# A two-layer graph network on one core: the last two expert blocks under a condition, and the experts' outputs taken by chunks from two queues

## The chip, the core and the metric

The kernel runs on one core of a Trainium2 chip. The metric is the device time of one execution in microseconds. A core has TensorE (PE, with its weight loads as PEld), VectorE (DVE), ScalarE (ACT), GpSimd (POOL) and SyncE (SP), each with an instruction order of its own, and 16 DMA engines that SP, ACT and POOL feed through queues. SBUF is the on-chip memory of 128 partitions, PSUM the one that TensorE writes.

## The reference, cut to what matters

3125 nodes with 256 features go through two layers of a graph network with mixers and mixtures of experts. The change lies where layer 0 ends and layer 1 begins:

```python
# layer 0, expert part: x is the layer norm of the nodes, 8 experts of width 1024, the best 2 of each node
shared = gelu(x @ W1s + b1s) @ W2s + b2s
rw = softmax(x @ Wr); topw, topi = top_k(rw, 2); topw = topw / sum(topw)
mask = sum(one_hot(topi, 8) * topw[..., None], axis=-2)
priv = gelu(einsum('bsd,edf->bsef', x, W1p) + b1p) @ W2p + b2p        # per expert
x_out = x_in + shared + einsum('bsed,bse->bsd', priv, mask)
# layer 1, messages: 50000 edges, 4 heads of 64 features
xn = layernorm(x_out)
messages = (xn @ W_forward.T)[src] * dir[:, 0:1] + (xn @ W_reverse.T)[src] * dir[:, 1:2]
# attention scores per edge, softmax over the edges of a target, weighted sum per target
```

Layer 1 has a second, linear attention (called galerkin in the kernel) over the same `xn`, and a mixture of experts whose router is a graph attention over 32768 edges of its own.

## The kernel before, in words

`self.x` holds the nodes in SBUF as 25 tiles of 125 rows by 256. CHUNKS cuts the 25 tiles into seven chunks of 4, 4, 4, 4, 3, 3 and 3 tiles. The framework decides the order of instructions on each engine from a cost model and from the order of the program, except inside `tc.manual_schedule(engines=...)`, where the named engines keep the order of the program.

**Experts of layer 0** (`layer0_ffn`). A counting pass on VectorE gives every pair of node and expert a slot. Each expert's slots are rounded up to blocks of BLK = 256 rows; `nb` is the number of blocks of each expert and `end` its running sum. NBLK = 2 * 3125 // 256 + 8 = 32 blocks is what any routing can need at most. Rows are scattered to their slots in device memory. The loop over the blocks then does, for every block b:

- `block_in`: SP reads the block's expert from `exi` and loads the block's rows (L847), W1 (L848), W2 (L849) and the bias (L850); three buffers each.
- `block_hidden`: four transposes (L858), a copy to `xs` on VectorE (L859), products with W1 (L864) with a gelu on ScalarE each (L866), and some small VectorE operations that compute the weights `own` and the target rows `toi` (L870 to L884). A slot that no node uses gets a spare row as its target.
- `block_out` of the block before (or, in block 0, the last chunk of the shared expert): products with W2 (L892), the weighting `yo` on VectorE (L895), and two scatters of 128 rows into y2 in device memory on POOL (L58, told apart by their names: `y<-yo,toi`).
- `sort_columns`: eight more scatters on POOL (`sorted<-s_rows,pos`), which carry out a part of the sort of layer 1's own edges, 256 columns in all. It fills a buffer `s_rows` (L1054; 16 buffers) and writes the block's `toi` into it (L1055), which ties the scatters to the pace of the blocks.

After the loop, y2 holds for each node its two experts' outputs, in two halves of 3125 rows. For each chunk and each half SP loads the rows (L67, the helper `move`, two DMAs of 112 and 13 partitions) into one of three buffers per half, and VectorE adds them to `self.x` (L915).

**Start of layer 1** (`layer1_mix`). `layernorm` goes over the chunks: statistics on VectorE (L168, L169), Sqrt on ScalarE (L170), reciprocal and normalised rows on VectorE (L171, L178), transposes on TensorE (L183), copies to `xT` on ScalarE (L185). After that, per tile, the product of `xT` with both message weights (`token_matmul`, L191), a copy on ScalarE (L1189), and per chunk two DMAs of SP into the table `tab1` (L67, `tab<-t_st`). The message loop begins with `fetch`: POOL gathers rows of `tab1` by the edges' sources (L51, `g<-tab,t_src`), 391 gathers in groups of eight; the weights of the linear attention (`nat`, L1451) are loaded and transposed meanwhile.

Two conditionals are there before the change, L476 and L1360: paths for edges in any order, whose test `bad > 0` is false for these inputs.

Of the kernel before, what the change touches and what calls it, by code (L numbers as in the profile page):

```python
# [8 lines left out]
F32 = mybir.dt.float32  # L9
I32 = mybir.dt.int32  # L10
BF16 = mybir.dt.bfloat16
AF = mybir.ActivationFunctionType
OP = mybir.AluOpType
AX = mybir.AxisListType
PSUM = bass.MemoryType.PSUM
DRAM = bass.MemoryType.DRAM

N = 3125
D = 256
P = 125  # L20
NT = 25
# [7 lines left out]
NBLK = 2 * N // BLK + 8  # L29
# [33 lines left out]
def move(queue, out, in_):  # L63


    for s in (slice(0, 112), slice(112, P)):
        queue.dma_start(out[s], in_[s])  # L67
# [7 lines left out]
def rows_of(table):  # L75
    return table.rearrange("(t p) d -> p t d", p=P)
# [12 lines left out]
class Kernel:  # L89
# [596 lines left out]
    def layer0_ffn(self):  # L686
        nc, tc, a = self.nc, self.tc, self.a
        NE, FC = 8, 8
        with ExitStack() as c:
# [70 lines left out]
            exi = keep.tile([1, NBLK], I32, name="exi")  # L760
            nc.vector.tensor_copy(exi, exf)


# [133 lines left out]

            todo = None
            for b in range(NBLK):
                ins = block_in(b)  # L900
                nxt = block_hidden(b, *ins)
                if b == 0:
                    output(*pending)
                else:
                    block_out(*todo)
                self.sort_columns(hp, b * EC // NBLK, (b + 1) * EC // NBLK, nxt[3])
                todo = nxt
            block_out(*todo)

            for t0, n in CHUNKS:  # L910
                s = slice(t0, t0 + n)
                for i in range(2):
                    r = wp.tile([P, 4, D], F32, name=f"w{i + 1}")
                    move(nc.sync, r[:, :n, :], rows_of(self.y2[i * N:(i + 1) * N])[:, s, :])
                    nc.vector.tensor_add(self.x[:, s, :], self.x[:, s, :], r[:, :n, :])  # L915

# [132 lines left out]
    def sort_columns(self, pool, f0, f1, pace):  # L1049


        nc = self.nc
        rows = pool.tile([128, EC // NBLK, 16], I32, name="s_rows", bufs=16)
        nc.vector.tensor_copy(rows[:, :f1 - f0, :], self.src2[:, f0:f1, None].to_broadcast([128, f1 - f0, 16]))  # L1054
        nc.vector.tensor_copy(rows[:, :f1 - f0, 15], pace[:, 0:1].to_broadcast([128, f1 - f0]))  # L1055
        for f in range(f0, f1):
            self.unordered("sorted", scatter(nc, self.sorted[:], self.pos2[:, f:f + 1], rows[:, f - f0, :]))
# [110 lines left out]
    def layer1_mix(self):  # L1168
        nc, tc, a = self.nc, self.tc, self.a
        W, HD = 68, 64  # L1170
        with ExitStack() as m:
            big = m.enter_context(tc.tile_pool(name="l1", bufs=1))
            wk = m.enter_context(tc.tile_pool(name="l1w", bufs=2))
# [5 lines left out]

            xT = big.tile([128, 2, N], F32, name="xT2")  # L1180
            tab1 = self.tab1 = self.dram.tile([N, 2 * W], F32, name="tab1")
            with tc.tile_pool(name="l1l", bufs=1) as lp:
                self.layernorm(lp, ps_a, "2", xT)
            for t0, n in CHUNKS:
                st = wk.tile([P, 4, 2 * W], F32, name="t1_st")
                for i in range(n):
                    pm = ps_a.tile([P, 2 * W], F32, name="ln_pt")
                    self.token_matmul(pm, xT, t0 + i, self.wcat)
                    nc.scalar.copy(st[:, i, :], pm)  # L1189
                move(nc.sync, rows_of(tab1)[:, t0:t0 + n, :], st[:, :n, :])  # L1190

# [112 lines left out]

            E_ = mybir.EngineType
            with tc.manual_schedule(engines={E_.PE, E_.DVE, E_.Activation}):
# [38 lines left out]
            for t0, n in CHUNKS:  # L1345
                s = slice(t0, t0 + n)
                for t in range(t0, t0 + n):
                    for h in range(4):
                        xs = self.x[:, t, h * HD:(h + 1) * HD]
                        nc.vector.scalar_tensor_tensor(xs, acc[:, t, h, :HD], den[:, t, h:h + 1], xs,  # L1350
                                                       op0=OP.mult, op1=OP.add)
        self.layer1_any_order()

    def layer1_any_order(self):
# [573 lines left out]
```

## Time and profile before

| What | us |
|---|---|
| median of 3 runs (2807.82 to 2812.39) | 2810.51 |
| the profiled execution | 3210.01 |
| its span, first to last instruction | 3208.3 |
| its first block's products to its last scatter of y2 | 1293.5 to 1792.8 |
| its first load of y2 to the first gather of messages | 1794.3 to 1865.4 |
| its mean granted TensorE clock | 0.844 |

The profiled execution is about 400 us longer than the runs without a profile; durations in the text are from the profiled one. A row of a group or of the timeline gives the line, the engine, the operation, output <- inputs and shape; "[2.50 <-DVE yo L895]" means that the engine had stood idle for 2.50 us and what ended that. A queue (SPq, POOLq) is where an engine's DMAs, branches and semaphore instructions are recorded. A digit at the end of a tile's name is left out in the profile, so y2 is `y`, `xT2` is `xT`, `tab1` is `tab` and `t1_st` is `t_st`.

### The profile page before, as it was taken

The numbers are of one execution on the slowest core, as the hardware profiler recorded it, in microseconds if no ns is written. First come the engines' busy times: TensorE is split into PE (matmuls) and PEld (weight loads), VectorE is DVE, ScalarE is ACT, GpSimd is POOL, SyncE is SP. The second block draws the span as 40 slices with busy tenths as digits, with TensorE's granted clock in tenths as the row PEclk, the third lists the DMA queues.
The fourth block names the chain that finished last, engine by engine and source line by source line (L and its number), as shares of the span: only waits on it lengthen the run. The fifth ranks groups of instructions, "written<-read, shape, count | busy, mean of one in ns | idle before, by whom it ended". The sixth has DMA issues, their size and how long they took to land. (4 is left out here: it accounts for less than half of the span.)

```text
span 3208.3 us, 26947 instructions
## 1 busy us (share of the span) xinstructions
PE 2295.1 (72%) x9183; PEld 1705.1 (53%) x9183; DVE 1516.4 (47%) x3630; ACT 539.8 (17%) x1107; POOL 1640.0 (51%) x1490
## 2 busy tenths in 40 slices
PE   1753652169998699899999458798668564788773
PEld 1442431057675466788787345465546353555552
DVE  7874750065547760122111448688569810122225
ACT  1420000000000111222222124344000110122213
POOL 5887887700000170566666157777547246555612
PEclk9865765579998699999999779899878777989886
DMA  8904200034330020655554422221112210111133
GB/s 311 367 2 112 68 12 1 0 78 98 79 98 29 17 76 1 211 169 184 180 177 150 100 69 49 45 48 44 40 31 46 68 37 7 21 33 43 41 90 72
DMA packets 179585, 265.05 MB, mean 83 GB/s; under 512 B 54288, under 2 KB 143866, under 8 KB 176051
## 3 DMA queue, kind: packets, MB, share of 16 engines
q1 hardware_dynamic: 121057, 206.38, 21.1%
q0 software_dynamic: 52480, 47.70, 7.2%
q10 hardware_dynamic: 5894, 9.09, 0.8%
q8 instruction: 76, 1.25, 0.2%
q14 instruction: 78, 0.63, 0.1%
HBM read 178.73 MB, written 84.21 MB: 82 GB/s over the span
## 5 line engine op out<-in xcount | busy, mean ns | idle before, releaser
L51 POOL DMA_INDIRECT g<-tab,t_src x391 | 454.4, 1162 | 259.1 <-issue 111.4
L58 POOL DMA_INDIRECT adj<-ch_sum,ch_place x391 | 488.8, 1250 | 148.0 <-issue 119.4
L460 PE MATMUL psum<-sup,adjT 125*125 125x256 f32 x1250 | 328.2, 411 | 218.6 <-issue 164.5
L460 PEld LDWEIGHTS psum<-sup,adjT 125*125 125x125 f32 x1250 | 250.8, 203 | 285.2 <-issue 200.6
L58 POOL DMA_INDIRECT sorted<-s_rows,pos x256 | 245.9, 961 | 187.6 <-DVE s_rows L1055 119.1
L51 POOL DMA_INDIRECT G<-tabg,g_src x256 | 251.2, 981 | 159.5 <-DVE g_src L1613 83.9
L1286 PE MATMUL pw<-v,hot 128*125 128x260 f32 x1244 | 328.4, 427 | 0.0
L1286 PEld LDWEIGHTS pw<-v,hot 128*125 128x125 f32 x1244 | 259.0, 212 | 50.5
L1644 PE MATMUL fpy<-fw,fh 128*125 128x256 f32 x800 | 208.5, 418 | 86.8 <-ACT fh L1638 36.9
L864 PE MATMUL ph<-xs,w 128*128 128x256 f32 x1024 | 232.3, 385 | 33.4 <-issue 29.6
L1644 PEld LDWEIGHTS fpy<-fw,fh 128*125 128x125 f32 x800 | 164.5, 209 | 135.9 <-ACT fh L1638 43.4
L864 PEld LDWEIGHTS ph<-xs,w 128*128 128x128 f32 x1024 | 194.2, 192 | 71.3 <-issue 44.0
L892 PE MATMUL py<-w,h 128*128 128x256 f32 x1024 | 231.2, 379 | 0.0
L463 DVE TENSOR_TENSOR x<-x,psum 125x512 f32<-125x512 f32 (+1 forms) x104 | 69.1, 666 | 327.2 <-remote 169.4
L1636 PE MATMUL fph<-xT,fw 128*128 128x500 f32 (+1 forms) x448 | 181.2, 553 | 37.0 <-ACT fh L1638 34.0
L892 PEld LDWEIGHTS py<-w,h 128*128 128x128 f32 x1024 | 192.1, 190 | 24.8
L620 POOL MEMSET tier<- 125x64 f32 x1 | 0.2, 157 | 378.1 <-PE psum L460 378.1
L866 ACT ACTIVATE h<-ph,b 128x256 f32<-128x256 f32 x256 | 121.2, 474 | 392.4 <-PE ph L864 357.4
L1030 PE MATMUL pctx<-s_mv,s_ro 128*128 128x256 f32 x512 | 154.9, 413 | 1.9 <-DVE s_mv L1029 1.9
L1636 PEld LDWEIGHTS fph<-xT,fw 128*128 128x128 f32 x448 | 86.2, 195 | 111.8 <-issue 52.8
L170 ACT ACTIVATE ln_rs<-ln_mv,eps 125x4 f32<-125x4 f32 (+1 forms) x28 | 7.5, 296 | 793.0 <-DVE ln_mv L169 793.0
L1638 ACT ACTIVATE fh<-fph,cols 128x500 f32<-128x500 f32 (+1 forms) x112 | 69.5, 633 | 420.4 <-PE fph L1636 226.5
(524 smaller groups left out, 3435.7 us busy)
## 6 DMA issues: line engine op xcount, KB each, us to landing
adjT<-adj SPq DMA_DIRECT2D x25, 1367.2 KB
adj<-zero SPq DMA_DIRECT2D x22, 1536.0 KB
w<-in_L_ffn_W1p_dram SPq DMA_DIRECT2D x32, 1024.0 KB
w<-in_L_ffn_W2p_dram SPq DMA_DIRECT2D x32, 1024.0 KB
slots<-empty SPq DMA_DIRECT2D x1, 8448.0 KB
srow<-slots SPq DMA_DIRECT2D x32, 264.0 KB
adj<-ch_sum,ch_place POOLq DMA_INDIRECT x391
g<-tab,t_src POOLq DMA_INDIRECT x391
```

Of the source, the lines that this page charges most:

```text
L51: nc.gpsimd.indirect_dma_start(out=out, out_offset=None, in_=table, in_offset=bass.IndirectOffsetOnAxis(ap=idx, axis=0))
L58: return nc.gpsimd.indirect_dma_start(out=table, out_offset=bass.IndirectOffsetOnAxis(ap=idx, axis=0), in_=rows, in_offset=None, **kw)
L460: nc.tensor.matmul(pm[:, i, :], mats[b][:, (a0 + i) * P:(a0 + i + 1) * P], sup[:, b, :], start=(b == b0), stop=(b == b0 + n - 1))
L463: nc.vector.tensor_add(xs, xs, pm[:, :m, :])
L864: nc.tensor.matmul(ph, w1[:, k, f * 128:(f + 1) * 128], xs[:, k, :], start=(k == 0), stop=(k == 1))
L866: nc.scalar.activation(h[:, f, :], ph, AF.Gelu, bias=b1[:, f:f + 1])
L892: nc.tensor.matmul(py, h[:, f, i * 128:(i + 1) * 128], w2[:, f, :], start=(f == 0), stop=(f == FC - 1))
L1030: nc.tensor.matmul(p1, ro[:, f - f0, :], mv, **st)
L1286: nc.tensor.matmul(pw.rearrange("p h c -> p (h c)"), hot[:, i - i0, :], v[:, i, :, :].rearrange("p h c -> p (h c)"), start=(i == i0), stop ...
L1636: nc.tensor.matmul(ph[:, :n * P], w1[:, k, f * 128:(f + 1) * 128], xT[:, k, t0 * P:(t0 + n) * P], start=(k == 0), stop=(k == 1))
L1638: nc.scalar.activation(hs[:, f, :n * P], ph[:, :n * P], AF.Gelu, bias=self.col("L1_ffn_b1", ei * FC + f))
L1644: nc.tensor.matmul(py, hs[:, f, i * P:(i + 1) * P], w2[:, f, :], start=(f == 0), stop=(f == FC - 1))
```

## The change

- NBLK - 2 = 30 blocks run without a condition. The last two stand in `tc.If(many > 30)`, where `many` is the number of blocks that the routing needs, kept in a tile `blocks` and loaded into a register of every engine. In the conditional each block's load, hidden part and output follow each other.
- The 256 sort columns are spread over 30 blocks: the first block carries 24, the others eight, and `s_rows` is filled in pieces of eight columns.
- The loads of y2 and their sums, layer 1's norm, its transposes and the message products move into a new function `experts_in`, in which PE, DVE, ACT and SP keep the order of the program. All loads are issued ahead, one half of y2 from SP's queue and the other from ACT's, into seven buffers. Each chunk goes through sum and statistics (`moments`), and one chunk later through normalising, transposes, products and the write to `tab1` (`table`).
- The normalised rows are computed on ScalarE (Identity with scale and bias per partition) instead of VectorE.

```diff
--- before.py
+++ after.py
@@ -759,6 +759,8 @@
             nc.vector.tensor_reduce(exf, which[:, :, 1:], AX.X, OP.add)
             exi = keep.tile([1, NBLK], I32, name="exi")
             nc.vector.tensor_copy(exi, exf)
+            blocks = keep.tile([1, 1], I32, name="blocks")
+            nc.vector.tensor_copy(blocks, end[:1, NE - 1:NE])
 
 
             nc.vector.tensor_sub(run, run, cnt)
@@ -895,24 +897,26 @@
                     nc.vector.tensor_scalar(yo, py, own[:, i, 2:3], None, op0=OP.mult)
                     self.unordered("y2", scatter(nc, self.y2[:], to[:, i:i + 1], yo))
 
-            todo = None
-            for b in range(NBLK):
+
+            sure = NBLK - 2
+            early = 24
+            todo, f1 = None, 0
+            for b in range(sure):
                 ins = block_in(b)
                 nxt = block_hidden(b, *ins)
                 if b == 0:
                     output(*pending)
                 else:
                     block_out(*todo)
-                self.sort_columns(hp, b * EC // NBLK, (b + 1) * EC // NBLK, nxt[3])
+                f0, f1 = f1, early + (EC - early) * b // (sure - 1)
+                for f in range(f0, f1, 8):
+                    self.sort_columns(hp, f, min(f + 8, f1), nxt[3])
                 todo = nxt
             block_out(*todo)
-
-            for t0, n in CHUNKS:
-                s = slice(t0, t0 + n)
-                for i in range(2):
-                    r = wp.tile([P, 4, D], F32, name=f"w{i + 1}")
-                    move(nc.sync, r[:, :n, :], rows_of(self.y2[i * N:(i + 1) * N])[:, s, :])
-                    nc.vector.tensor_add(self.x[:, s, :], self.x[:, s, :], r[:, :n, :])
+            many = nc.values_load(blocks[0:1, 0:1], min_val=0, max_val=NBLK)
+            with tc.If(many > sure):
+                for b in range(sure, NBLK):
+                    block_out(*block_hidden(b, *block_in(b)))
 
 
     def digit_ranks(self, pool, psum, key, bins):
@@ -1050,7 +1054,7 @@
 
 
         nc = self.nc
-        rows = pool.tile([128, EC // NBLK, 16], I32, name="s_rows", bufs=16)
+        rows = pool.tile([128, 8, 16], I32, name="s_rows", bufs=16)
         nc.vector.tensor_copy(rows[:, :f1 - f0, :], self.src2[:, f0:f1, None].to_broadcast([128, f1 - f0, 16]))
         nc.vector.tensor_copy(rows[:, :f1 - f0, 15], pace[:, 0:1].to_broadcast([128, f1 - f0]))
         for f in range(f0, f1):
@@ -1169,6 +1173,15 @@
         nc, tc, a = self.nc, self.tc, self.a
         W, HD = 68, 64
         with ExitStack() as m:
+            E_ = mybir.EngineType
+            xp = m.enter_context(tc.tile_pool(name="l1x", bufs=1))
+            xT = xp.tile([128, 2, N], F32, name="xT2")
+            tab1 = self.tab1 = self.dram.tile([N, 2 * W], F32, name="tab1")
+            with tc.tile_pool(name="l1l", bufs=1) as lp, \
+                    tc.tile_pool(name="l1lp", bufs=3, space=PSUM) as pl, \
+                    tc.tile_pool(name="l1lm", bufs=4, space=PSUM) as pm, \
+                    tc.manual_schedule(engines={E_.PE, E_.DVE, E_.Activation, E_.SP}):
+                self.experts_in(lp, pl, pm, xT)
             big = m.enter_context(tc.tile_pool(name="l1", bufs=1))
             wk = m.enter_context(tc.tile_pool(name="l1w", bufs=2))
             gp = m.enter_context(tc.tile_pool(name="l1g", bufs=3))
@@ -1177,17 +1190,6 @@
             ps_w = m.enter_context(tc.tile_pool(name="l1pw", bufs=4, space=PSUM))
             ps_s = m.enter_context(tc.tile_pool(name="l1ps", bufs=1, space=PSUM))
 
-            xT = big.tile([128, 2, N], F32, name="xT2")
-            tab1 = self.tab1 = self.dram.tile([N, 2 * W], F32, name="tab1")
-            with tc.tile_pool(name="l1l", bufs=1) as lp:
-                self.layernorm(lp, ps_a, "2", xT)
-            for t0, n in CHUNKS:
-                st = wk.tile([P, 4, 2 * W], F32, name="t1_st")
-                for i in range(n):
-                    pm = ps_a.tile([P, 2 * W], F32, name="ln_pt")
-                    self.token_matmul(pm, xT, t0 + i, self.wcat)
-                    nc.scalar.copy(st[:, i, :], pm)
-                move(nc.sync, rows_of(tab1)[:, t0:t0 + n, :], st[:, :n, :])
 
 
             late = big.tile([128, 1], F32, name="late")
@@ -1302,7 +1304,6 @@
                         nc.scalar.copy(unit[:, w, :], big2[:P, 0, :])
 
 
-            E_ = mybir.EngineType
             with tc.manual_schedule(engines={E_.PE, E_.DVE, E_.Activation}):
                 todo = self.galerkin(big, wk, ps_a, ps_c, xT)
                 starts = [(j0, min(GROUP, NJ - j0)) for j0 in range(0, NJ, GROUP)]
@@ -1350,6 +1351,61 @@
                         nc.vector.scalar_tensor_tensor(xs, acc[:, t, h, :HD], den[:, t, h:h + 1], xs,
                                                        op0=OP.mult, op1=OP.add)
         self.layer1_any_order()
+
+    def experts_in(self, pool, psum, psum_m, xT):
+
+
+
+        nc, W = self.nc, 68
+        mv = pool.tile([P, NT, 2], F32, name="ln_mv2")
+        rs = pool.tile([P, 2, NT], F32, name="ln_rs2")
+        y2 = self.y2[:2 * N].rearrange("(i t p) d -> p i t d", i=2, p=P)
+        loads = []
+        for t0, n in CHUNKS:
+            r = pool.tile([P, 2, 4, D], F32, name="y_in", bufs=len(CHUNKS))
+            for i, queue in enumerate((nc.sync, nc.scalar)):
+                move(queue, r[:, i, :n, :], y2[:, i, t0:t0 + n, :])
+            loads.append(r)
+
+        def moments(r, t0, n):
+            s = slice(t0, t0 + n)
+            for i in range(2):
+                nc.vector.tensor_add(self.x[:, s, :], self.x[:, s, :], r[:, i, :n, :])
+            st = pool.tile([P, 4, 6], F32, name="ln_st2", bufs=2)
+            for t in range(t0, t0 + n):
+                nc.vector.bn_stats(st[:, t - t0, :], self.x[:, t, :])
+                nc.vector.bn_aggr(mv[:, t, :], st[:, t - t0, :])
+            nc.scalar.activation(rs[:, 0, s], mv[:, s, 1], AF.Sqrt, bias=self.eps[:P])
+
+        def table(t0, n):
+            s = slice(t0, t0 + n)
+
+            nc.vector.reciprocal(rs[:, 0, s], rs[:, 0, s])
+            nc.vector.scalar_tensor_tensor(rs[:, 1, s], mv[:, s, 0], -1.0, rs[:, 0, s], op0=OP.mult, op1=OP.mult)
+            row = pool.tile([P, 4, D], F32, name="ln_row2", bufs=2)
+            for i in range(n):
+                t = t0 + i
+                nc.scalar.activation(row[:, i, :], self.x[:, t, :], AF.Identity, bias=rs[:, 1, t:t + 1],
+                                     scale=rs[:, 0, t:t + 1])
+            for k in range(2):
+                pt = psum.tile([128, 4, P], F32, name="ln_pt")
+                for i in range(n):
+                    nc.tensor.transpose(pt[:, i, :], row[:, i, k * 128:(k + 1) * 128], self.ident[:P, :P])
+                nc.scalar.copy(xT[:, k, t0 * P:(t0 + n) * P], pt[:, :n, :].rearrange("p a b -> p (a b)"))
+            st = pool.tile([P, 4, 2 * W], F32, name="t1_st", bufs=2)
+            for i in range(n):
+                pm = psum_m.tile([P, 4, 65], F32, name="pw").rearrange("p h c -> p (h c)")[:, :2 * W]
+                self.token_matmul(pm, xT, t0 + i, self.wcat)
+                nc.scalar.copy(st[:, i, :], pm)
+            move(nc.sync, rows_of(self.tab1)[:, t0:t0 + n, :], st[:, :n, :])
+
+        before = None
+        for r, chunk in zip(loads, CHUNKS):
+            moments(r, *chunk)
+            if before is not None:
+                table(*before)
+            before = chunk
+        table(*before)
 
     def layer1_any_order(self):
```

## The prediction

> **What bounds the kernel now.** I read the page first, then stages, then the order of time inside the two stages that are edited. The page says only that no engine is full over the whole program.
>
> ```profile
> span 3208.3 us, 26947 instructions
> PE 2295.1 (72%) x9183; PEld 1705.1 (53%) x9183; DVE 1516.4 (47%) x3630; ACT 539.8 (17%) x1107; POOL 1640.0 (51%) x1490
> ```
>
> So the stages decide. The windows view (columns: length, then PE, PEld, DVE, ACT, POOL busy, granted clock, DMA share, GB/s) shows the expert blocks full on TensorE, and then a hole of 71 us, here cut into loads, norm and message products:
>
> ```profile
> 1600.00:1700.00 100.00, 94.18 (x438) 80.98 (x437) 16.99 (x78) 25.97 (x56) 61.97 (x65) 0.99 0.55 184
> ...
> 1794.00:1824.00 30.00, 0.00 (x0) 0.00 (x0) 15.53 (x16) 0.00 (x0) 0.29 (x2) 0.50 1.03 234
> 1824.00:1846.20 22.20, 11.71 (x51) 8.59 (x51) 19.39 (x83) 9.66 (x22) 0.00 (x0) 0.58 0.01 4
> 1846.20:1865.40 19.20, 15.05 (x100) 13.27 (x100) 0.00 (x0) 8.20 (x27) 0.01 (x1) 0.94 0.34 89
> ```
>
> The three steps of the hole run one after the other: DMA at share 1.03, then VectorE (19.4 of 22.2 us), then the products. The timeline has its two ends, the copies that open each block, and the first instruction that needs the message table:
>
> ```profile
> 1754.51 0.68 DVE L859 COPY xs<-ln_pt 128x512 f32<-128x512 f32 x1
> 1770.17 0.68 DVE L859 COPY xs<-ln_pt 128x512 f32<-128x512 f32 x1
> 1791.85 0.96 POOL L58 DMA_INDIRECT y<-yo,toi  x1 [2.50 <-DVE yo L895]
> 1794.27 23.55 SPq L67 DMA_DIRECT2D w<-y  x28
> 1798.80 1.23 DVE L915 TENSOR_TENSOR x<-x,w 125x1024 f32<-125x1024 f32 x1 [4.08 <-DMA w<-y]
> 1865.39 0.99 POOL L51 DMA_INDIRECT g<-tab,t_src  x1 [70.41 <-DMA tab<-t_st]
> ```
>
> A block takes 15.66 us (1770.17 - 1754.51), and from the first load of y2 to the first gather it is 1865.39 - 1794.27 = 71.1 us. POOL stood still for 70.4 us of it, and everything of layer 1 comes after: what is saved here reaches the end.
>
> **What the skill says.** (1) "DMA: Bandwidth & Descriptors", section "Issuing engines are not separate DMA queues": loads from two engines run on the same 16 DMA engines, and a second queue saves issue time only. The trace agrees: the first 12 of the 28 loads are issued within 5 us, and afterwards the adds come 2.1 us apart for 0.5 MB each at a DMA share above 1. (2) "ScalarE: Activation LUTs", section "Table sets: the hidden batching unit": identity and copy lie in every table set. In the trace Sqrt and Copy alternate from 1826.4 to 1862.3 us after a single table load; Identity between them is not shown. (3) "Runtime: NRT & Kernel Launch", section "Instruction fetch mechanics": a taken branch to code outside the fetched window stalls its engine. The trace agrees: the branches of the two conditionals that are there (L476, L1360) took PE 3.76 and 3.46 us, the other engines 0.05 to 0.07.
>
> **Part 1: two blocks less.** Block count is a matter of data. Computed from the reference's router, the eight experts get 771, 726, 534, 750, 1090, 772, 775 and 832 rows; rounded up to blocks of 256 that is 4+3+3+3+5+4+4+4 = 30. The test is 30 > 30, so the two blocks are skipped; the nearest way to 31 is the expert with 750 rows getting 769. Everything a block issues goes with it: 64 matmuls, 8 gelus, 4 weight DMAs on SP, 2 scatters on POOL, the latter two beside TensorE. Worth 2 x 15.66 = **-31.3 us**. The tail (last product to the last scatter at 1791.85) stays the same.
>
> **Part 2: the sort's scatters.** All 256 must now go beside 30 blocks: 24 in block 0, then 8 per block. Extra in block 0: 16 scatters at 1.265 us (0.96 and 0.30 of issue) = 20 us on POOL. In the trace POOL idles 5.9, 2.8, 2.5 and 1.0 us between block 0 and its third sort, and starts that one at 1326.0; with the change it would have done 32 columns and two outputs by about 1335, where before it had 24 and two. That is nearly level. But the loop hangs on POOL through VectorE:
>
> ```profile
> DVE s_rows L1054 <- DMA sorted<-s_rows,pos: 180.9, 16, 11.9
> ```
>
> Sixteen times VectorE waits at L1054 for a row buffer that a scatter still reads (16 buffers), and the previous block's `yo` and this block's `xs` stand behind it, so TensorE does too. Where that copy is put in the order of block 1 or 2, the extra scatters could hold TensorE from 1323.7 to about 1335. Bounds 0 and 12 us; I take **+2**, since the extra scatters also push back the moment at which the copy can be placed.
>
> **Part 3: the conditional.** For L476 and L1360 the trace gives the price at a join:
>
> ```profile
>   DVE ln_st L168: 3.5, 1
> ...
> L1360 POOLq INC_SWDGE_SEM  x1: 2324/2324/2324, 2510.4 to 2510.4; - x1
> ```
>
> The first is VectorE's idle time after L476; at L1360 it was 1.8 us. On POOL the last gather ended at 2508.5 and its semaphore work at 2512.7, 4.2 us later. Here PE, DVE and ACT have nothing to do until the first rows of y2 have landed, so their branches, PE's 3.5 us included, are hidden under about 9 us of load and add. SP passed its last weight load at 1755 and waits anyway. What counts is POOL: y2 may be read only once POOL has accounted for the skipped scatters: 1792.8 + 4.2 = 1797.0, against 1794.27 before. I take **+3**; bounds 0 (it overlaps the landing of the last scatter) and 6.
>
> **Part 4: chunks through the hole.** T is the first load's issue. Loads: 6.4 MB at the same 246 GB/s, 26 us, both halves of a chunk together every 4.3 us. The first add came 4.5 us after the first issue, the second 2.1 later: chunk 0 is complete at T+6.7, chunk 1 at T+11.0. VectorE per chunk of four: two adds at 1.23, four statistics at 0.39: 4.1 us, under the load's 4.3. Chunk 1's statistics end at T+15.0; after its Sqrt, reciprocal and product the first `table` starts at **T+15.5**.
>
> From there ScalarE sets the pace, since its order is fixed by hand and each round goes to TensorE and back twice. Normalising moved from VectorE (0.35 each) to ScalarE, with two pointer operands. The page "ScalarE: Activation LUTs", section "What ACT_TABLE_LOAD costs", gives 186 + 2 x 93 + 0.833 x 256 = 585 ns, 93 of it overlapped: an estimate of 0.49 (the same formula without pointers gives 399; the trace's Square at L609 has 400). A round of four, by the trace otherwise:
>
> - Sqrt of the next chunk 0.25, four rows 4 x 0.49 = 2.0
> - last row to the first xT copy, through the transposes: 0.91 (1834.56 to 1835.47)
> - two xT copies 1.05
> - end of copy to the first product's copy: 0.05 + 0.77 = 0.8 (1857.34 to 1858.11)
> - four product copies, paced by TensorE's 0.6: 0.27 + 1.8 = 2.1
>
> Together 7.2; for three tiles 5.9. Sum 4 x 7.2 + 3 x 5.9 = 46.5 us. The last copy to the first gather was 3.1 us (1862.28 to 1865.39). So the first gather comes at T + 15.5 + 46.5 + 3.1 = T+65.1 against T+71.1: **-6 us** only. The chunks do overlap with the load, but ScalarE's rounds don't overlap each other. Bounds: load-bound at T+26 plus one round and the write, T+40 (-31); or ScalarE held by its own 14 load issues. Twelve issues took SP 5 us, so I expect 14 to end by T+8, ahead of the first Sqrt; were they drawn out to the length of the load, the first Sqrt would come at T+24 and the gather about 10 later (+4).
>
> The weight loads of the message stage (`nat`, issued at 1818.55) now follow the table's writes on SP; the cover is 15 us from the first gather to their use at 1880.8, against about 4 for the load (0.5 MB at 246 GB/s and the latency of a first load).
>
> **Sum.** -31.3 + 2 + 3 - 6 = **-32 us** on the profiled execution of 3210.0 us (span 3208.3). That execution is 14% longer than the median of 2810.5. The removed blocks ran at a granted clock of 0.99 and are TensorE time, so I carry the sum over unscaled: **2778 us**. Scaled down it would be -28.
>
> **Rivals.**
>
> *R1, the rounds overlap better* (waits on TensorE shorter than taken, loads faster than 246 GB/s, as the 349 GB/s of the loads' first microsecond allow): first gather at T+45 to T+58, total -39 to -52. Against it: one instruction order per engine. Chance 0.13.
>
> *R2, the small prices are all dear*: the sort holds TensorE 12, the join 6, ScalarE is held by its loads (+4 instead of -6): -31 + 12 + 6 + 4 = -9; halves of it give -20. For it: L1054's waits. Chance 0.19.
>
> *R3, slower: ScalarE reloads its tables.* If Identity and Sqrt didn't share a set, each of seven rounds would switch twice: 14 x 2.66 us by that page's price (1.28 of it is the load, as at 1826.39) = 37 us in the very chain that decides: -32 + 37 = +5. It decides from about 32 us on, so the bare 1.28 each (18 us) would not turn the sign. Against it: (2) above. Chance 0.03.
>
> *R4, the change doesn't skip*: with 31 blocks or more both would run behind the branch, unpipelined: 2.1 MB of weights at 246 GB/s, 9 us and 2 of latency, then 14 us of products, the second 15.7: 41 us instead of 31, total +9. The count speaks against it. Chance 0.02.
>
> **Numbers.** Forecast -32 (-25 to -39) 0.61, R1 0.13, R2 0.19, R3 0.03, R4 0.02, near zero 0.02. Within 0.2% (5.6 us) is about what a measurement of this kernel can't tell from no change. Range: 2763 (-48, most of R1) to 2797 (-13, half of R2 and more). Faster 0.93, same 0.02, slower 0.05.
>
> **What would show it.** Right: 960 records at each of L864 and L892, no instruction of the skipped blocks, y2's loads 2 to 5 us after the last scatter has landed, ScalarE's rows, xT copies and product copies in rounds of 6 to 7 us, first gather 60 to 68 us after the first load. Part 2 is wrong if the third block starts later than 1327. Wrong altogether: table loads between rounds, records of block 31, or a first gather beyond T+75.

## The result and the profile after

The changed kernel takes 2796.9 us (median of 8 runs, 2788.2 to 2800.1) against 2807.0 us of the kernel before in the same comparison (8 runs): a ratio of 0.9961, 95% interval 0.9948 to 0.9974. That is about 10 us less (7 to 15); the forecast was 32 less. The direction was right, two thirds of the gain did not come. That 2796.9 still lies at the upper edge of the range given, 2763 to 2797, is luck: the kernel before took 3.5 us less in this comparison than in the three runs from which the forecast was counted (2810.5).

The head of the page of the changed kernel:

```profile
span 2798.4 us, 26658 instructions
PE 2201.9 (79%) x9047; PEld 1657.6 (59%) x9047; DVE 1508.4 (54%) x3589; ACT 544.0 (19%) x1116; POOL 1659.7 (59%) x1486
```

The skipped blocks are gone (9183 - 9047 = 136 records of PE, two times 64 products and 4 transposes). But the span can't be set against the 3208.3 us of the first profile: that one lay 400 us above the medians, this one lies close to them. So the kernel before was profiled again (run `before_short` below), in an execution of 2810 us, and stages are compared with that one. Three numbers are read: the first `xs` copy, the first load of y2, the first gather. From the first to the second is the **loop**, from the second to the third the **hole**; the time from one `xs` copy to the next is a block's **period**. The profiles of `e1_even` and `e3_no_if` are of slow executions (3227 and 3253 us); all ratios rest on fast runs alone.

| us | loop | hole | both |
|---|---|---|---|
| before (`before_short`) | 478.4 | 73.3 | 551.7 |
| after | 464.9 | 76.4 | 541.3 |
| after, second profile (`after_again`) | 466.8 | 73.5 | 540.3 |

What comes ahead of the loop (1072.6 in both) and after the first gather (1184.3 and 1184.5) is the same. The loop got only 13.5 us shorter although two blocks are missing, and the hole, which was to lose 6, got no shorter. The two ends of the hole in `before_short`:

```profile
1551.06 24.46 SPq L67 DMA_DIRECT2D w<-y  x28
1624.34 0.99 POOL L51 DMA_INDIRECT g<-tab,t_src  x1 [72.57 <-DMA tab<-t_st]
```

The windows view of the changed kernel (length; PE, PEld, DVE, ACT, POOL busy; granted clock, DMA share, GB/s), a full stretch of blocks and then the hole in three parts:

```profile
1400.00:1500.00 100.00, 100.00 (x472) 86.22 (x472) 19.23 (x88) 26.03 (x55) 65.85 (x69) 1.00 0.54 185
1537.50:1560.50 23.00, 0.00 (x0) 0.00 (x0) 8.98 (x20) 0.00 (x0) 0.00 (x0) 0.50 1.03 240
1560.50:1582.50 22.00, 15.56 (x61) 11.76 (x62) 16.90 (x44) 13.60 (x31) 0.00 (x0) 0.66 0.26 66
1582.50:1613.90 31.40, 21.68 (x91) 16.92 (x89) 4.62 (x16) 15.38 (x41) 0.14 (x2) 0.66 0.15 37
```

The blocks run TensorE full, as they do in `before_short` (100.00 of 100 us there too). In the first 23 us of the hole ScalarE's busy time is 0.00: nothing of norm or products overlaps the loads. The timeline of the same kernel says why (start, length; in brackets the idle time and its releaser):

```profile
1513.08 0.69 DVE L861 COPY xs<-ln_pt 128x512 f32<-128x512 f32 x1
1534.77 0.96 POOL L58 DMA_INDIRECT y<-yo,toi  x1 [2.50 <-DMA y<-yo,toi]
1537.50 21.53 SPq L67 DMA_DIRECT2D y_in<-y  x14
1537.74 22.82 ACTq L67 DMA_DIRECT2D y_in<-y  x14
1544.11 2.48 DVE L1373 TENSOR_TENSOR x<-x,y_in 125x1024 f32<-125x1024 f32 x2 [9.62 <-DMA y_in<-y]
1560.58 1.28 ACT L1378 ACT_TABLE_LOAD   x1 [39.05 <-DMA y_in<-y]
1562.62 2.08 ACT L1388 ACTIVATE ln_row<-x,ln_rs 125x256 f32<-125x256 f32 x4 [0.26 <-DVE ln_rs L1384]
1613.86 0.98 POOL L51 DMA_INDIRECT g<-tab,t_src  x1 [0.94 <-issue]
```

ScalarE (ACTq) is issuing its 14 loads from 1537.74 to 1560.56. Chunk 0's two additions started at 1544.11, yet its Sqrt stands behind the last load in ScalarE's order: table load at 1560.58, 23.1 us after the first load.

The second loss is at the start of the loop, again in the timeline of the changed kernel:

```profile
1087.76 0.23 DVE L1058 COPY s_rows<-src 128x128 int32<-128x128 int32 x1 [9.25 <-DMA sorted<-s_rows,pos]
1095.81 0.46 DVE L1058 COPY s_rows<-src 128x128 int32<-128x128 int32 x1 [6.62 <-DMA sorted<-s_rows,pos]
1095.95 0.68 DVE L861 COPY xs<-ln_pt 128x512 f32<-128x512 f32 x1
1096.73 1.62 PE L866 MATMUL ph<-xs,w 128*128 128x256 f32 x3 [11.92 <-issue]
1104.98 0.23 DVE L1058 COPY s_rows<-src 128x128 int32<-128x128 int32 x1 [8.35 <-DMA sorted<-s_rows,pos]
1118.74 0.23 DVE L1058 COPY s_rows<-src 128x128 int32<-128x128 int32 x1 [13.53 <-DMA sorted<-s_rows,pos]
1118.88 0.87 DVE L897 TENSOR_SCALAR yo<-py,own 128x256 f32<-128x256 f32 x2
1119.64 0.96 POOL L58 DMA_INDIRECT y<-yo,toi  x1 [5.73 <-DVE yo L897]
1119.66 0.69 DVE L861 COPY xs<-ln_pt 128x512 f32<-128x512 f32 x1
```

and the same stretch of VectorE in `before_short`, the two fills and the two `xs` copies (blocks 1 and 2) alone:

```profile
1088.09 0.23 DVE L1054 COPY s_rows<-src 128x128 int32<-128x128 int32 x1 [8.46 <-DMA sorted<-s_rows,pos]
...
1089.26 0.68 DVE L859 COPY xs<-ln_pt 128x512 f32<-128x512 f32 x1
1100.64 0.23 DVE L1054 COPY s_rows<-src 128x128 int32<-128x128 int32 x1 [10.70 <-DMA sorted<-s_rows,pos]
...
1105.14 0.69 DVE L859 COPY xs<-ln_pt 128x512 f32<-128x512 f32 x1
```

In the changed kernel the `xs` of block 1 (1095.95) and the `yo` ahead of the `xs` of block 2 (1119.66) stand on VectorE behind fills of `s_rows`, and these wait for scatters. TensorE had been idle for 11.92 us when block 1 began. The first three block periods are 23.4, 23.7 and 16.1 us; in `before_short` they are 16.6, 15.9 and 14.5.

### The profile page after: what moved, and what is told of

Its sections match the earlier page's. It is cut to its first block, busy times and chain, and to the rows that moved or that the text cites. A ratio compares the mean times of both kernels' runs of the same rounds, so it can differ in the third digit from the quotient of the medians.

```text
span 2798.4 us, 26658 instructions
## 1 busy us (share of the span) xinstructions
PE 2201.9 (79%) x9047; PEld 1657.6 (59%) x9047; DVE 1508.4 (54%) x3589; ACT 544.0 (19%) x1116; POOL 1659.7 (59%) x1486
## 3 DMA queue, kind: packets, MB, share of 16 engines
q1 hardware_dynamic: 114273, 198.43, 23.1%
## 5 line engine op out<-in xcount | busy, mean ns | idle before, releaser
L58 POOL DMA_INDIRECT adj<-ch_sum,ch_place x391 | 505.9, 1294 | 152.8 <-issue 109.7
L460 PE MATMUL psum<-sup,adjT 125*125 125x256 f32 x1250 | 294.1, 395 | 50.9 <-DMA adjT<-adj 39.6
L460 PEld LDWEIGHTS psum<-sup,adjT 125*125 125x125 f32 x1250 | 241.8, 195 | 92.7 <-DMA adjT<-adj 36.4
L866 PE MATMUL ph<-xs,w 128*128 128x256 f32 x960 | 219.3, 387 | 22.9 <-issue 20.5
L866 PEld LDWEIGHTS ph<-xs,w 128*128 128x128 f32 x960 | 183.2, 193 | 58.2 <-issue 31.0
L894 PE MATMUL py<-w,h 128*128 128x256 f32 x960 | 216.7, 379 | 0.0
L1700 PE MATMUL fpy<-fw,fh 128*125 128x256 f32 x800 | 186.2, 389 | 32.9 <-DVE y L1702 28.0
L1700 PEld LDWEIGHTS fpy<-fw,fh 128*125 128x125 f32 x800 | 152.6, 192 | 70.4 <-DVE y L1702 29.2
L894 PEld LDWEIGHTS py<-w,h 128*128 128x128 f32 x960 | 180.1, 190 | 23.3
L58 POOL DMA_INDIRECT slots<-rows,abi x50 | 74.3, 1485 | 100.2 <-DVE r_cum L948 85.3
L897 DVE TENSOR_SCALAR yo<-py,own 128x256 f32<-128x256 f32 x60 | 27.8, 481 | 190.8 <-PE py L894 190.8
```

What stands on the lines that cost most here:

```text
L58: return nc.gpsimd.indirect_dma_start(out=table, out_offset=bass.IndirectOffsetOnAxis(ap=idx, axis=0), in_=rows, in_offset=None, **kw)
L460: nc.tensor.matmul(pm[:, i, :], mats[b][:, (a0 + i) * P:(a0 + i + 1) * P], sup[:, b, :], start=(b == b0), stop=(b == b0 + n - 1))
L866: nc.tensor.matmul(ph, w1[:, k, f * 128:(f + 1) * 128], xs[:, k, :], start=(k == 0), stop=(k == 1))
L894: nc.tensor.matmul(py, h[:, f, i * 128:(i + 1) * 128], w2[:, f, :], start=(f == 0), stop=(f == FC - 1))
L1700: nc.tensor.matmul(py, hs[:, f, i * P:(i + 1) * P], w2[:, f, :], start=(f == 0), stop=(f == FC - 1))
```

## The experiments

The first four runs went to a chip on which every kernel, the one before too, takes about 3200 us; the others to one where that kernel takes 2807 us. Ratios are to the kernel before on the same chip. The changed kernel itself was not timed on the first chip; the nearest to it there is `e3_no_if`. T is the first load of y2, as in the prediction.

**`before_again`**: the kernel before, unchanged.

> The kernel before, unchanged, for a second profile. Theory A: the first profile of it was of a long execution (3210 us against a median of 2807), and in an execution near the median the block loop is shorter, about 14.5 us a block as in the changed kernel and not 15.66, so that the two blocks are worth 29 us and the block loop some 480 us. Rival B: blocks take 15.1 to 15.7 us again, and the shorter ones of the changed kernel are an effect of the change. The hole from the first load of y2 to the first gather should be 71 us in both.

Span 3191.9 us, loop 502.3, hole 72.8, periods of 15.1 to 15.7 us: like the first profile. On this chip that is the normal case, so the run said nothing on the executions of 2810 us. That was open until `before_short`.

**`e1_even`**: the 256 columns spread evenly over the 30 blocks, eight or nine each, none ahead.

```diff
-                f0, f1 = f1, early + (EC - early) * b // (sure - 1)
-                for f in range(f0, f1, 8):
-                    self.sort_columns(hp, f, min(f + 8, f1), nxt[3])
+                f0, f1 = f1, EC * (b + 1) // sure
+                self.sort_columns(hp, f0, f1, nxt[3])
...
-        rows = pool.tile([128, 8, 16], I32, name="s_rows", bufs=16)
+        rows = pool.tile([128, 9, 16], I32, name="s_rows", bufs=16)
```

> The changed kernel with the 256 sort columns spread evenly, 8 or 9 in each of the 30 blocks, instead of 24 in the first. Theory A: VectorE's waits at s_rows for POOL in the first three blocks held TensorE about 16 us; without them blocks 1 and 2 start 16 us apart as before, and the kernel is 12 to 16 us faster than the changed one (ratio to before about 0.991). Rival B: TensorE would have waited there for weights anyway, and the 9-column blocks cost POOL as much later: within 3 us of the changed kernel (0.995 to 0.997).

Ratio 0.9987 (0.9959 to 1.0016). The stall at the start was gone (16.6 and 17.4 us for the first periods, where `e3_no_if` has 29.5 and 30.5 on this chip), but most later periods rose to between 15.6 and 17.1 (near 15.1 in `e3_no_if`), and the loop took 499.5 us against 493.4. GpSimd's own work would fit into a period: 9 scatters of the sort and 2 into y2, 11 x 1.265 = 13.9 us. But in a block with nine columns the first y2 scatter stands behind the nine (at 1630.64 in one), the second `yo` came 2.9 us later with the next `xs` behind it, and TensorE idled 2.5 us; what that `yo` waited for the profile doesn't name. So the front-loading is the stall at the start, and columns spread this way cost the later blocks as much, which was rival B's second half; the later part rests on this one profile.

**`e2_sp_only`**: both halves of y2 from SP's queue.

```diff
-            for i, queue in enumerate((nc.sync, nc.scalar)):
+            for i, queue in enumerate((nc.sync, nc.sync)):
```

> The changed kernel with both halves of y2 loaded from SP's queue. Theory A: ScalarE was held until 23 us after the first load because its own queue took its 14 loads only as fast as data moved; freed, its first Sqrt comes at about 12 us and the first gather 65 us after the first load instead of 76: 10 us faster than the changed kernel (ratio to before about 0.992). Rival B: the loads are late on one queue, or the rounds stall later for data: first gather 74 us or more after the first load, no gain.

Ratio 0.9956 (0.9933 to 0.9979), where `e3_no_if` has 0.9988: about 8 us by the medians. The hole is 63.0 us (73.5 to 78.5 in the runs with two queues), and ScalarE's table load comes 10.4 us after the first load. ScalarE's own queue had held it. The 0.992 that was expected did not come; it was counted from the changed kernel's ratio on the other chip.

**`e3_no_if`**: the four lines of the conditional are taken out; for these inputs the same work remains.

> The changed kernel without the conditional: the last two blocks are left out of the program, which for these inputs computes the same. Theory A: the join costs the 2 to 3 us between the landing of the last scatter and the first load, so 1 to 3 us faster than the changed kernel. Rival B: the conditional also keeps work from moving across it and costs 6 us or more; or it costs nothing, because the loads wait for the last scatter's landing anyway.

Ratio 0.9988 (0.9968 to 1.0009), hole 73.5, the stall at the start is still there. The conditional isn't where the time went. In the profile of the changed kernel the records of L917, the conditional's line, give the same answer:

```profile
L917 PEldq COMPARE_BRANCH  x1: 347/347/347, 1531.3 to 1531.3; - x1
L917 POOLq INC_SWDGE_SEM  x1: 758/758/758, 1532.6 to 1532.6; - x1
```

TensorE's branch took 0.35 us and GpSimd's semaphore work 0.76 us. From the end of the last scatter into y2 to the first load it is 1537.50 - 1535.73 = 1.8 us, against 1.5 in `before_short`; but without the conditional, here, it is 1.8 us as well, and with it but the old loads (`e9_blocks_only`) 1.5 us. The 0.3 us belong to the new loads.

**`after_again`**: the control for the next three.

> The changed kernel, unedited, as the control of the next three. Theory A (the change gives the two skipped blocks, and loses part of that twice: the 16 scatters more in block 0 hold VectorE at the row buffers and TensorE behind it, and ScalarE is held behind its own loads of y2): first two block periods 23 to 30 us each where the kernel before has 16, then 14.5 to 15.1; first load of y2 to first gather 75 to 77 us; time 7 to 12 us under the kernel before. Rival B (the profile of the changed kernel was an odd execution): first periods near 16, or a hole of 66 to 71 us.

2797.5 us, ratio 0.9964 (0.9950 to 0.9978); first periods 23.2, 24.2 and 17.5, as theory A has it; hole 73.5, a little below what was expected.

**`e5_tail_sort`**: eight columns in each of the 30 blocks, the last 16 after the conditional.

```diff
-                f0, f1 = f1, early + (EC - early) * b // (sure - 1)
-                for f in range(f0, f1, 8):
-                    self.sort_columns(hp, f, min(f + 8, f1), nxt[3])
+                self.sort_columns(hp, 8 * b, 8 * b + 8, nxt[3])
...
+            for f in range(8 * sure, EC, 8):
+                self.sort_columns(self.edges, f, f + 8, todo[3], 2)
```

> Only the sort's schedule is changed: 8 columns in each of the 30 blocks and the last 16 columns after the conditional, beside the loads of y2. Theory A: the first two periods fall to 15 to 17 us and no later one rises above 15.7, so the loop is 14 to 20 us shorter than in after_again; the 16 scatters at the end cost POOL 20 us inside a hole of which POOL is free for 70, so the hole stays at 75 to 77 us; in all -14 to -20 us against after_again. Rival B (the 16 scatters are merely moved: their bytes or POOL's semaphore work delay the first gather or the loads of y2): the hole rises to 85 us or more and the total is within 6 us of after_again.

2797.3 us, ratio 0.9957 (0.9941 to 0.9974): nothing gained against `after_again`. The first part of the expectation came true: periods 16.6, 16.1 and 14.5, and from the first `xs` to the last only 424.8 us instead of 442.3. The second part did not: the whole loop is only 2.9 us shorter (463.9), and the hole is 78.5. The timeline of `e5_tail_sort`, PE's last products and GpSimd around them:

```profile
1499.48 0.95 POOL L58 DMA_INDIRECT sorted<-s_rows,pos  x1 [1.04 <-DVE s_rows L1059]
...
1504.93 13.11 PE L894 MATMUL py<-w,h 128*128 128x256 f32 x60
...
1522.20 0.96 POOL L58 DMA_INDIRECT sorted<-s_rows,pos  x1 [0.30 <-issue]
1523.46 0.96 POOL L58 DMA_INDIRECT y<-yo,toi  x1 [0.30 <-issue]
...
1529.77 0.96 POOL L58 DMA_INDIRECT sorted<-s_rows,pos  x1 [0.30 <-issue]
...
1533.57 0.96 POOL L58 DMA_INDIRECT y<-yo,toi  x1 [0.30 <-issue]
```

TensorE was done at 1518.0, but the framework had put the 16 scatters ahead of the last y2 scatters (probably because their data is ready earlier), and the last of these came at 1533.6, 36.4 us after the last `xs` instead of 21.7. Neither theory had said this: the scatters are still in front of what decides, only at the loop's other end. The hole is 5.0 us longer than in `after_again`, 4.2 of them in the rounds (48.7 us against 44.5), at a lower granted clock of TensorE; the last section comes back to it.

**`e6_tail_sp`**: `e5_tail_sort` with the edit of `e2_sp_only`.

> As e5_tail_sort, and both halves of y2 are loaded from SP's queue. Theory A: ScalarE is free from the first load on, its first Sqrt comes at about 12 us after the first load instead of 23, the hole is 62 to 66 us, and the total is another 10 to 14 us under e5_tail_sort (24 to 34 under after_again). Rival B (the single queue issues later, so that chunks arrive later, and the scatters of the tail now share the DMA engines with it): hole 70 us or more, within 5 us of e5_tail_sort.

2788.0 us, ratio 0.9932 (0.9915 to 0.9948): 9.3 us under `e5_tail_sort`, near the 10 to 14 expected, but 9.5 under `after_again` instead of 24 to 34, as `e5_tail_sort` had gained nothing. The hole is 62.6. Its timeline:

```profile
1533.63 24.91 SPq L67 DMA_DIRECT2D y_in<-y  x28
1543.93 1.28 ACT L1378 ACT_TABLE_LOAD   x1 [40.99 <-DVE ln_mv L1377]
1548.65 2.08 ACT L1388 ACTIVATE ln_row<-x,ln_rs 125x256 f32<-125x256 f32 x4
1596.26 0.98 POOL L51 DMA_INDIRECT g<-tab,t_src  x1 [0.85 <-issue]
```

One queue takes 24.9 us for all 28 loads, the two together took 23.1. ScalarE's table load comes 10.3 us after the first load instead of 23.1, the first rows at T+15.0, the gather at T+62.6.

**`e7_staged`**: `e6_tail_sp`, and ScalarE's work staged by one more chunk.

```diff
+        for i in range(C + 2):
+            if i < C:
+                moments(loads[i], *CHUNKS[i])
+            if 0 <= i - 1 < C:
+                row = rows(*CHUNKS[i - 1])
+            if 0 <= i - 2:
+                store = product(*CHUNKS[i - 2])
+                store()
+            if 0 <= i - 1 < C:
+                transposes(*CHUNKS[i - 1], row)
```

> As e6_tail_sp, with ScalarE's order staged by one more chunk: in each round the rows of chunk c are followed by the product copies and the write of chunk c-1, and only then by the xT copies of chunk c, so that ScalarE doesn't stand still while TensorE transposes and multiplies. Theory A (the rounds are latencies between ScalarE and TensorE in series): rounds fall from about 6.8 to about 5 us (ScalarE's own work: 0.25 + 2.0 + 1.05 + 4 x 0.27 to 0.9), the hole to 48 to 56 us, 8 to 15 us under e6_tail_sp. Rival B (TensorE's products at the low granted clock, 0.9 us each, are the pace): rounds stay at 6 to 7 us, one round more is added by the staging, and the hole is 63 to 70 us, not below e6_tail_sp.

2772.7 us, ratio 0.9877 (0.9860 to 0.9893): the best kernel here, 36 us under the kernel before (by the medians) and 25 under the changed one. The hole is 47.9 us. The windows view of `e7_staged`, hole alone:

```profile
1535.30:1551.00 15.70, 0.00 (x0) 0.00 (x0) 9.43 (x23) 2.03 (x4) 0.00 (x0) 0.50 1.03 216
1551.00:1583.20 32.20, 24.89 (x150) 19.80 (x150) 20.61 (x58) 24.93 (x69) 0.10 (x1) 0.87 0.62 147
```

and two of its rounds on ScalarE:

```profile
1555.73 2.08 ACT L1388 ACTIVATE ln_row<-x,ln_rs 125x256 f32<-125x256 f32 x4
1557.71 0.76 ACT L1409 COPY t_st<-pw 125x136 f32<-125x136 f32 x4
1558.52 1.05 ACT L1397 COPY xT<-ln_pt 128x500 f32<-128x500 f32 x2
1560.39 0.30 ACT L1378 ACTIVATE ln_rs<-ln_mv,eps 125x4 f32<-125x4 f32 x1 [0.82 <-DVE ln_mv L1377]
1560.71 2.08 ACT L1388 ACTIVATE ln_row<-x,ln_rs 125x256 f32<-125x256 f32 x4
```

A round is 1560.71 - 1555.73 = 5.0 us, the later ones 2.7 to 4.0. The four product copies take 0.76 us in one go: the products are ready when ScalarE comes to them, where in the changed kernel each copy waited for its own. ScalarE is busy in 24.93 of 32.20 us and TensorE in 24.89; neither is full. Part of the gain may lie in TensorE's granted clock, 0.87 over these 32 us against 0.77 over the rounds of `e6_tail_sp`: the new order brings both, and no run separates them.

**`before_short`**: the kernel before, for a profile near the medians.

> The kernel before, unedited, for a profile beside the next three. If its span is near the medians (about 2810) it gives the stages that the first profile couldn't: theory A expects a block period of 14.4 to 14.7 us once the loop is steady, first two periods of about 16, and 476 to 482 us from the first block's copy to the first load of y2; the hole at 70 to 73 us. Rival B (a block costs 15.1 to 15.7 us whatever the execution): 500 us and more for the loop.

Span 2808.6 us, loop 478.4, hole 73.3, first periods 16.6 and 15.9, steady ones 14.45: theory A. Two of its `xs` copies:

```profile
1512.50 0.69 DVE L859 COPY xs<-ln_pt 128x512 f32<-128x512 f32 x1
1526.95 0.69 DVE L859 COPY xs<-ln_pt 128x512 f32<-128x512 f32 x1
```

**`e9_blocks_only`**: the conditional blocks and the front-loaded sort, with loads, sum, norm and products as before.

> Only the conditional blocks and the front-loaded sort of the change; loads, sum, norm and products of the experts' outputs stay as in the kernel before. Theory A (two blocks give 29, the front-loaded scatters take 16 back, the conditional takes under 1): the loop is 12 to 14 us shorter than the loop of the kernel before, hole 70 to 73 us; time 10 to 15 us under the kernel before, which is somewhat more than the whole change. Rival B (the blocks give nearly 31, and it is the part with the chunks that takes 20 back): 25 us or more under the kernel before.

2794.9 us, ratio 0.9954 (0.9937 to 0.9972); loop 466.5, hole 72.3, first periods 23.4, 24.2, 17.4. This half alone gives about the whole of the change's gain.

**`e10_part4`**: only the part with the chunks and two queues; 32 blocks with eight columns each, without a condition.

> Only the part with the chunks and two queues of the change; all 32 blocks run without a condition, with 8 columns of the sort each. Theory A (ScalarE is held by its own load queue): hole 73 to 77 us against 70 to 73 before, loop as in the kernel before, so 2 to 6 us slower than before or within 0.2%. Rival B: the part with the chunks alone gains the 6 us that were forecast, with a hole of 63 to 67 us, because without a conditional the loads start at once.

2810.8 us against 2806.5, ratio 1.0011 (1.0003 to 1.0019); loop 478.9, hole 77.2. This half alone costs 3 to 4 us; ScalarE's table load comes 23.4 us after the first load here too.

**`e8_late_tail`**: `e7_staged`, with the last 16 scatters behind the last scatters into y2.

```diff
-            block_out(*todo)
+            last = block_out(*todo)
...
+            end_of = self.edges.tile([128, 1], I32, name="end_of")
+            nc.vector.tensor_copy(end_of, last[:, :1])
             for f in range(8 * sure, EC, 8):
-                self.sort_columns(self.edges, f, f + 8, todo[3], 2)
+                self.sort_columns(self.edges, f, f + 8, end_of, 2)
```

> As e7_staged, but the last 16 scatters of the sort take their pace from the last block's weighted output, so that they stand behind the last scatters into y2 on GpSimd instead of ahead of them. Theory A (in e5_tail_sort to e7_staged those 16 scatters held back the last y2 scatters by 16 us after TensorE's last product): the last scatter into y2 comes 21 to 23 us after the last block's xs copy instead of 36, the hole stays at 48 to 51 us since GpSimd is free in it, the time is 11 to 15 us under e7_staged. Rival B (the scatters then run beside the loads of y2, delay their landing and VectorE's first add): hole 55 us or more, within 6 us of e7_staged.

2776.4 us, ratio 0.9889 (0.9872 to 0.9905): not under `e7_staged`. The last y2 scatter came 21.7 us after the last `xs`, as theory A had it, and the hole stayed at 47.4. But the loads began late. Its timeline:

```profile
1517.62 0.96 POOL L58 DMA_INDIRECT y<-yo,toi  x1 [2.49 <-DMA y<-yo,toi]
1538.34 0.96 POOL L58 DMA_INDIRECT sorted<-s_rows,pos  x1 [0.30 <-issue]
1540.77 3.54 SPq L67 DMA_DIRECT2D y_in<-y  x8
```

and its view of waits for SP's queue over the end of the loop (us in total, times, the longest, counted from SP's last work before):

```profile
SPq L67 <- DMA sorted<-s_rows,pos: 53.0, 5, 48.1
```

By this view the first load has waited for scatters of the sort, whose data it doesn't read: 22.2 us from the last y2 scatter's end. Why it waits for them no run here shows. Putting the scatters behind the loads in the order of the program as well was not measured; an estimate of its worth is the 15 us by which `e7_staged` takes longer from the last `xs` to the first load (39.1 us) than the changed kernel does (24.4).

## Why the prediction was wrong, step by step

Two steps failed: Part 2's "I take **+2**" for the sort's scatters, which cost 16.2 us, and Part 4's "I expect 14 to end by T+8", where ScalarE's 14 load issues ended at T+23. Together they are worth about 24 us. Parts 1 and 3 nearly cancel, and 22 were missing.

| Step | Forecast | Shown by | Measured |
|---|---|---|---|
| Part 1, two blocks | -31.3 | steady period of `before_short` and after | -28.9 (2 x 14.45) |
| Part 2, sort's scatters | +2 (0 to 12) | first three periods, 63.2 - 47.0 | +16.2 |
| Part 3, conditional | +3 (0 to 6) | last scatter to first load, with and without it | 0 |
| Part 4, chunks | -6 | hole, 76.4 - 73.3, and 0.3 ahead of it | +3.4 (+0.5 in `after_again`) |
| Sum | -32 | loop and hole together | -9.3; the two profiles differ by 10.4 |

Of the 1.1 us that are left over, 0.9 are two longer periods in the middle of the loop of `before_short` (15.01 and 14.77) that the changed kernel doesn't have. The halves add up roughly: in loop and hole `e9_blocks_only` has -12.9 against `before_short`, `e10_part4` +4.4, together -8.5.

**Part 2 is the largest miss, and beyond its own bounds.** I had seen the mechanism, VectorE's wait at the row buffers with `yo`, `xs` and TensorE behind it, but placed one such wait. The changed kernel has several close together, as each piece of eight columns has a fill of its own and block 0 has three pieces. Each of these fills comes 1.2 to 4.8 us after GpSimd has ended the eighth scatter of a piece (1083.6, 1093.7, 1103.8 and 1113.9; then the fills at 1087.8, 1095.8, 1105.0 and 1118.7), and a piece takes GpSimd 8 x 1.265 = 10.1 us. In `before_short` one fill stands ahead of each early `xs` (1088.1, 1100.6, 1118.7); in the changed kernel two stand ahead of `xs` of block 1 (1087.8 and 1095.8) and two more ahead of that of block 2 (1105.0 and 1118.7). My sum compared GpSimd's total of scatters at one moment and called it nearly level. It had to follow VectorE's order instead. The sign named for this part came: the third block starts 47.1 us after the first, where 36 was the limit (1327). `e5_tail_sort` shows it from the other side: with eight columns per block the first three periods take 47.2 us.

**Part 4 fell at a named step:** "Twelve issues took SP 5 us, so I expect 14 to end by T+8". They ended at T+23. The count was off too: in the first profile SP issued 10 loads in those 5.0 us, and the twelfth issue ended at T+7.1, so the slowing showed already. My bound for that case (first Sqrt at T+24, +4) is what came: T+23.1, and a hole longer by 3.1. The rest of that part's working holds: with the loads on SP alone (`e6_tail_sp`) the first rows come at T+15.0 (forecast T+15.5) and the gather at T+62.6 (T+65.1). In the changed kernel the seven rounds took 1610.2 - 1562.6 = 47.6 us (46.5), since most product copies came 0.9 us apart where 0.6 was taken. Two slips in that sum are small: the terms of a round add up to 7.1 and not 7.2, and the median of the Square at L609 is 417 ns, 398 its least. `e7_staged` then shows that the length of the rounds, which I had taken as given, depended on their order: 48 us of hole instead of 63.

**Part 1** was mis-sized by 2.4 us, because a period of 15.66 was taken from an execution 400 us longer than the median; "I carry the sum over unscaled" was the wrong choice. The reason given was that the blocks are TensorE time; but the prediction's own line has TensorE busy in 94.18 of 100 us there, and 15.66 x 0.94 = 14.7. **Part 3** was too dear by 3 us. TensorE's branch took 0.35 us and not the 3.5 and 3.8 of the two others, so the stall that the Trainium skill describes in "Runtime: NRT & Kernel Launch", section "Instruction fetch mechanics", for a taken branch outside the fetched window doesn't show here; whether this target lay outside it the record doesn't say.

**The rivals.** R2, the small prices all dear, came nearest in size (-9), in part by luck: one of its terms is absent (the join), and one is larger than its bound (the sort). R1 didn't happen in this order of instructions. R3 is excluded: one table load in the whole hole, with Sqrt, Identity and Copy alternating after it, as "ScalarE: Activation LUTs", section "Table sets: the hidden batching unit", has it for copy and identity. R4 is excluded: 960 records each at L866 and L894. The sign that I had named for a prediction wrong altogether, a first gather beyond T+75, appeared in one profile of the changed kernel (T+76.4) and not in the other (T+73.5).

## What to carry to other kernels

An engine that computes next should not issue the loads it waits for: here its first four issues took 2.1 us and all 14 as long as the data, 22.8. Before work is moved forward on an idle engine, follow the order of the engine that feeds it: the idle time of GpSimd was there, but the fills on VectorE stood ahead of TensorE's copies. And take durations from an execution near the median, or profile again before a sum of small terms is trusted.

## What was unexpected of the hardware

- The issues of loads go fast only at first. With two queues each issued four in about 2 us, then they went at the pace of the data: ScalarE had issued 8 by T+12, 14 by T+23, while the loads moved 240 GB/s. SP alone issued 11 in 6.5 us. The second queue shortened the issue of all loads from 24.9 to 23.1 us; that agrees with "DMA: Bandwidth & Descriptors", section "Issuing engines are not separate DMA queues", cited in the prediction.
- The same kernel takes 2807 us on one chip and 3200 on another; the first profile, 3210 us, looks like the latter. At the stages of this change that is 24 us in the loop and almost nothing in the hole (72.8 and 73.3).
- TensorE's granted clock in the second half of the hole was 0.66 in the changed kernel and 0.87 in `e7_staged`, where its work lies closer together. The length of the rounds goes with it: the same seven rounds took 48.7 us at a mean granted clock of 0.61 (`e5_tail_sort`), 48.2 at 0.64 (`e10_part4`), 47.6 at 0.68 (the changed kernel), 44.5 at 0.74 (`after_again`) and 44.1 at 0.77 (`e6_tail_sp`). Where the clock was 0.50, product copies came 0.91 us apart (from 1582.0 in the changed kernel); where it was 1.00, 0.46 (from 1583.4 in `after_again`). The rounds differ by 3.1 us between these two profiles of one kernel, the holes by 2.9. No run varied the clock alone.
